# A residual product over 128 samples: the second last sample is stored in four transfers of 49, 64, 8 and 7 rows instead of one of 128

## The chip, the cores and the metric

The kernel runs on one core of a Trainium2 chip. The metric is the device time of one execution in microseconds (us); the time before is the median of three runs. A profiled execution of the kernel stands beside them: its span runs from the first to the last instruction that the profiler recorded. The core has 16 DMA engines that move data between HBM and the on-chip memory (SBUF), and they are used by transfers that SyncE (SP) and ScalarE (ACT) issue. A transfer adds 16 to a semaphore when all of it has landed.

## The reference

For each of 128 samples a 128x1024 matrix `x[b]` is multiplied by one of eight 128x128 weight matrices, chosen by an index, and added to itself:

```python
def reference(x, itok_B_0_7, L0_cond_weights):   # x (128, 128, 1024) f32
    ...
    w = weights[subjects]                        # (128, 128, 128)
    out = jnp.einsum('bct,bcd->bdt', x, w)
    ...
    x = x + _L0_cond_ref(x, itok_B_0_7, L0_cond_weights)
    return x
```

Each sample is 512 KB in and 512 KB out, so 67 MB are read and 67 MB written.

## The kernel before, in words

The samples are taken in `NT` = 32 groups of four (`H` = 2 pairs of `G` = 2 samples). Group `i` lies in slot `i % 12` of twelve SBUF buffers `xs`, as 128 partitions (rows) of 4 x 1024 floats; one row of one sample is 4 KB. It is an order written out by hand, with semaphores:

- SP issues one load for each sample (`load`, through `transfer`, L57), in the order of the samples. From group 12 on it waits until the slot's former group has been stored.
- GpSimd (POOL) copies the weight matrix that the index names (L196), TensorE makes four products of 128x512 for each pair (L206), and VectorE adds the pair's product in PSUM to `xs` in place (L217) and raises `s_added`.
- ACT issues the stores (`store`, L57), in the order of the groups. Groups 1 to 30 are stored whole, 2 MB in one transfer; group 0 in two pairs of 1 MB; group 31, the last, in three: its first pair (samples 124 and 125, 1 MB), then sample 126 (512 KB), and, after the big critical section and on ACT's queue too, sample 127 (L231, 512 KB).

Sample 126 is left alone by the expression `q1 - (b == B - 1)` in the last turn of the loop, which takes sample 127 out of the pair's store; the last transfer is issued outside, since the end of the program waits for it. SP meanwhile runs through a list of waits (L227 to L229), one for each of the last twelve slots and one for group 31's first pair, and then the program's closing instructions.

A store of 128 rows is carried by all 16 DMA engines, each of which works off what the two queues (SP's loads and ACT's stores) have for it.

Of the kernel before, what the change touches and what calls it, by code (L numbers as in the profile page):

```python
# [30 lines left out]
G = 2  # L31
H = 2
# [3 lines left out]
SLOTS = 12  # L36
# [5 lines left out]
DMA = 16  # L42

IDLE = 3

ROWS = 4
QUEUES = {mybir.EngineType.SP: "qSPDynamicHW", mybir.EngineType.Activation: "qActDynamicHW"}
# [2 lines left out]
def transfer(nc, engine, out, in_):  # L50

    later, nc._always_lower_symbolic_ap = nc._always_lower_symbolic_ap, False
    ins, outs = engine.lower_ap_dma(in_), engine.lower_ap_dma(out)
    nc._always_lower_symbolic_ap = later
    return engine.add_instruction(  # L57
        mybir.InstDMACopy(
            name=nc.get_next_instruction_name(),
            engine=engine.engine,  # L60
            ins=ins,
            outs=outs,
            mode="Copy",
            cce_op=ALU.bypass,
            queue=QUEUES[engine.engine],
        )
    )


@with_exitstack  # L70
def kernel(
    ctx: ExitStack,
    tc: tile.TileContext,
    x: bass.AP,
    subjects: bass.AP,
    weights: bass.AP,
    out: bass.AP,
):
    nc = tc.nc
    B, C, T = x.shape  # L80
    S, _, D = weights.shape
    NT = B // (G * H)

    def sbuf(name, *shape, dtype=F32):
        return ctx.enter_context(nc.sbuf_tensor(name, list(shape), dtype)).ap()

    given, near, wrap, index = (
        sbuf(name, 1, B, dtype=I32) for name in ("given", "near", "wrap", "index")
    )
    w_all = sbuf("w_all", C, S, D)  # L90
    ws = [sbuf(f"w{i}", C, 1, D) for i in range(W_SLOTS)]
    zeros = sbuf("zeros", C, N)
    xs = [sbuf(f"x{i}", C, H * G, T) for i in range(SLOTS)]
    ps = [
        ctx.enter_context(nc.psum_tensor(f"ps{i}", [D, G, T], F32)).ap() for i in range(P_SLOTS)
    ]

    s_given = tc.alloc_semaphore("s_given")
    s_wall = tc.alloc_semaphore("s_wall")
    s_index = tc.alloc_semaphore("s_index")  # L100
    s_zeros = tc.alloc_semaphore("s_zeros")
    s_copied = tc.alloc_semaphore("s_copied")
    s_product = tc.alloc_semaphore("s_product")
    s_added = tc.alloc_semaphore("s_added")

    s_pair = [[tc.alloc_semaphore(f"s_pair{i}_{h}") for h in range(H)] for i in range(SLOTS)]


    s_first = tc.alloc_semaphore("s_first")

    def emptied(i, h):

        turns = i // SLOTS
        return (DMA * G + (DMA if h == H - 1 else 0)) * turns

    def loaded(i, q):

        h = q // G
        return s_pair[i % SLOTS][h], emptied(i, h) + DMA * G

    def load(engine, i, q):
        k, h = i % SLOTS, q // G
        transfer(
            nc,
            engine,
            xs[k][:, q, :],
            x[i * H * G + q].rearrange("(a r) t -> a (r t)", r=ROWS),
        ).then_inc(s_pair[k][h], DMA)

    def store(i, q0, q1):  # L130
        k, b = i % SLOTS, i * H * G
        transfer(
            nc,
            nc.scalar,
            out[b + q0 : b + q1].rearrange("g d t -> d g t"),
            xs[k][:, q0:q1, :].rearrange("d (o g) t -> d o (g t)", g=min(G, q1 - q0)),
        ).then_inc(s_first if i == 0 and q1 == G else s_pair[k][(q1 - 1) // G], DMA)

    with tc.tile_critical():  # L139

        nc.scalar.dma_start(given, subjects.rearrange("(o b) -> o b", o=1)).then_inc(s_given, DMA)

        nc.vector.memset(zeros, 0.0).then_inc(s_zeros, 1)  # L143
        nc.tensor.wait_ge(s_zeros, 1)
        for _ in range(IDLE):
            nc.tensor.matmul(  # L146
                ps[P_SLOTS - 1][:, G - 1, :N], zeros[:, :D], zeros, start=True, stop=True
            )

        nc.vector.wait_ge(s_given, DMA)
        nc.vector.tensor_scalar(near, given, -S, S - 1, ALU.max, ALU.min).then_inc(s_index, 1)  # L153
        nc.vector.wait_ge(s_index, 1)
        nc.vector.tensor_scalar(wrap, near, 0, S, ALU.is_lt, ALU.mult).then_inc(s_index, 1)  # L155
        nc.vector.wait_ge(s_index, 2)
        nc.vector.tensor_tensor(index, near, wrap, ALU.add).then_inc(s_index, 1)  # L157
        nc.gpsimd.wait_ge(s_index, 3)


        nc.sync.dma_start(w_all, weights.rearrange("s c d -> c s d")).then_inc(s_wall, DMA)  # L161
        for i in range(NT):
            k = i % SLOTS
            if i == SLOTS:
                nc.sync.wait_ge(s_first, DMA)
            if i >= SLOTS:
                nc.sync.wait_ge(s_pair[k][H - 1], emptied(i, H - 1))
            for q in range(H * G):
                load(nc.sync, i, q)


        for j in range(NT * H):
            i, q0, q1 = j // H, j % H * G, (j % H + 1) * G
            k = i % SLOTS
            p = ps[j % P_SLOTS]

            ahead = j < P_SLOTS
            if ahead:  # L180
                nc.tensor.wait_ge(*loaded(i, q0))
            for q in range(q0, q1):
                b = i * H * G + q
                if b % R == 0:
                    _, subject = nc.values_load_multi_w_load_instructions(
                        index[0:1, b : b + R],
                        engines=[mybir.EngineType.Pool],
                        min_val=0,
                        max_val=S - 1,
                        skip_runtime_bounds_check_because="the index is clamped on the chip above",  # L190
                    )
                if b == 0:
                    nc.gpsimd.wait_ge(s_wall, DMA)
                if not ahead and q == q0:
                    nc.gpsimd.wait_ge(s_added, j - P_SLOTS + 1)
                copy = nc.gpsimd.tensor_copy(  # L196
                    ws[b % W_SLOTS], w_all[:, bass.ds(subject[b % R], 1), :]
                )
                if not ahead and q == q0:
                    copy.wait_op(*loaded(i, q0), "sem-ge")  # L200
            copy.then_inc(s_copied, 1)

            nc.tensor.wait_ge(s_copied, j + 1)
            for q in range(q0, q1):
                for t in range(0, T, N):
                    mm = nc.tensor.matmul(  # L206
                        p[:, q % G, t : t + N],
                        ws[(i * H * G + q) % W_SLOTS][:, 0, :],
                        xs[k][:, q, t : t + N],
                        start=True,  # L210
                        stop=True,
                    )
            mm.then_inc(s_product, 1)

            mine = xs[k][:, q0:q1, :]
            nc.vector.wait_ge(s_product, j + 1)
            nc.vector.tensor_tensor(  # L217
                mine, p, mine, ALU.add
            ).then_inc(s_added, 1)

            if i == 0 or q1 == H * G or i == NT - 1:
                nc.scalar.wait_ge(s_added, j + 1)
                store(i, q0 if i in (0, NT - 1) else 0, q1 - (b == B - 1))

    with tc.tile_critical() as waits:  # L227
        for i in range(NT - SLOTS, NT):
            nc.sync.wait_ge(s_pair[i % SLOTS][H - 1], emptied(i + SLOTS, H - 1))  # L229
        nc.sync.wait_ge(s_pair[(NT - 1) % SLOTS][0], emptied(NT - 1 + SLOTS, 0) + DMA)  # L230
    last = nc.scalar.dma_start(out[B - 1], xs[(NT - 1) % SLOTS][:, H * G - 1, :])  # L231

    tc.add_manual_dep(
        last.ins,
        waits.name,
        mybir.DependencyInfo(mybir.DependencyClass.NoSync, mybir.DependencyReason.SCHED_ONLY),
        reason="the end of the program waits for it",
    )
# [27 lines left out]
```

## Time and profile before

| | us |
|---|---|
| median of 3 runs | 327.0 (326.23 to 327.02) |
| span of the profiled execution | 325.4 |
| last add of VectorE ends | 278.7 |
| L231, the last store, is issued | 305.0 |
| last store has landed | 324.4 |
| TensorE busy | 241.1 (74%) |
| VectorE busy | 147.9 (45%) |
| bytes moved | 134.85 MB, mean 414 GB/s |

The page divides the span into 40 slices of 8.1 us; a digit is the busy share in tenths. The DMA line is the mean over the core's 16 DMA engines, so that one busy engine alone shows as 0.06 in a table with two decimals. The queue numbers of the page are q1 for SP's transfers and q10 for ACT's; q8 and q14 fetch instructions. Of the stores the page lists the size and the median time from issue to landing:

```profile
out_dram<-x ACTq DMA_DIRECT2D x30, 2048.0 KB, 47.3
out_dram<-x ACTq DMA_DIRECT2D x3, 1024.0 KB, 13.9
out_dram<-x ACTq DMA_DIRECT2D x2, 512.0 KB, 21.1
```

The two transfers of 512 KB are those of samples 126 and 127. A transfer waits in the queue behind the earlier ones, which is why its time to landing is long beside its size.

### The profile page before, as it was taken

How to read it: one execution, taken by the hardware profiler on the slowest of the kernel's cores; microseconds unless marked ns; L12 is line 12 of the kernel's file. 1: busy time of each engine (PE TensorE's matmuls, PEld its weight loads, DVE VectorE, ACT ScalarE, POOL GpSimd, SP SyncE). 2: the span in 40 equal slices, each digit the busy share in tenths (PEclk: the TensorE clock that was granted, in tenths of full speed). 3: DMA queues.
4: the chain of work that ended last, by engine and by line, in shares of the span. 5: the costliest groups of instructions: out<-in, count | busy, mean ns of one | idle time of the engine just before them, and what ended most of it. 6: DMA issues, size and time to landing. Idle time of an engine off the chain costs nothing.

```text
span 325.4 us, 1606 instructions
## 1 busy us (share of the span) xinstructions
PE 241.1 (74%) x518; PEld 95.2 (29%) x518; DVE 147.9 (45%) x68; POOL 34.3 (11%) x132
## 2 busy tenths in 40 slices
PE   6999988988888888888888888888888689000000
PEld 2444332333333333333333333333333233000000
DVE  1375754555555555454555555554554544200000
POOL 1011111011111111111011111111111010000000
PEclk9999999999999999999999999999999889655555
DMA  6999999999999999999999999999999999999994
GB/s 250 413 418 421 428 425 422 420 428 427 426 421 427 429 415 427 424 431 423 423 435 417 416 432 424 428 417 428 433 419 424 418 437 415 429 425 427 426 428 201
DMA packets 16074, 134.85 MB, mean 414 GB/s; under 512 B 2625, under 2 KB 3650, under 8 KB 3906
## 3 DMA queue, kind: packets, MB, share of 16 engines
q1 hardware_dynamic: 7184, 67.64, 49.7%
q10 hardware_dynamic: 8882, 67.11, 49.1%
q8 instruction: 4, 0.07, 0.1%
q14 instruction: 4, 0.03, 0.0%
HBM read 67.63 MB, written 67.11 MB: 414 GB/s over the span
## 4 chain that ended last, share of the span: by engine, by line
PE 42%; DVE 20%; issue 16%; POOL 4%; DMA 2%; POOLq 1%; SPq 0%
PE ps L206 42%; DVE x L217 20%; POOL w L196 4%; DMA x<-in_x_dram 2%; POOLq L196 1%; SPq L57 0%; SPq L161 0%; POOLq L139 0%; SPq L262 0%; SPq L139 0%
## 5 line engine op out<-in xcount | busy, mean ns | idle before, releaser
L206 PE MATMUL ps<-x,w 128*128 128x512 f32 x512 | 236.1, 607 | 33.6 <-POOL w L196 32.1
L217 DVE TENSOR_TENSOR x<-ps,x 128x2048 f32<-128x2048 f32 x64 | 146.7, 2292 | 129.1 <-PE ps L206 129.1
L206 PEld LDWEIGHTS ps<-x,w 128*128 128x128 f32 x512 | 93.3, 191 | 176.6 <-issue 93.9
L196 POOL COPY w<-w_all 128x128 f32 x128 | 34.1, 296 | 238.0 <-DMA x<-in_x_dram 207.7
L146 PE MATMUL ps<-zeros 128*128 128x512 f32 x6 | 5.0, 992 | 1.7 <-DVE zeros L143 1.7
L146 PEld LDWEIGHTS ps<-zeros 128*128 128x128 f32 x6 | 1.8, 328 | 3.7 <-issue 2.1
L143 DVE MEMSET zeros<- 128x512 f32 x1 | 0.5, 485 | 1.1 <-SPq L139 1.1
L153 DVE TENSOR_SCALAR near<-given 1x128 int32<-1x128 int32 x1 | 0.2, 215 | 0.6 <-DMA given<-in_itok_B_dram 0.6
L157 DVE CUSTOM_DVE_ANT_0 index<-near,wrap 1x256 uint16<-1x256 uint16 x1 | 0.3, 278 | 0.0
L155 DVE TENSOR_SCALAR wrap<-near 1x128 int32<-1x128 int32 x1 | 0.2, 216 | 0.0
L253 POOL MEMSET const-float32-0.0<- 128x1 f32 x1 | 0.1, 99 | 0.2 <-issue 0.2
L253 POOL MEMSET const-bfloat16-1.0<- 128x1 bf16 x1 | 0.1, 102 | 0.0
L253 POOL MEMSET const-uint8-127<- 128x1 uint8 x1 | 0.1, 102 | 0.0
L253 POOL MEMSET const-float32-1.0<- 128x1 f32 x1 | 0.1, 99 | 0.0
## 6 DMA issues: line engine op xcount, KB each, us to landing
x<-in_x_dram SPq DMA_DIRECT2D x128, 512.0 KB, 32.3
out_dram<-x ACTq DMA_DIRECT2D x30, 2048.0 KB, 47.3
out_dram<-x ACTq DMA_DIRECT2D x3, 1024.0 KB, 13.9
out_dram<-x ACTq DMA_DIRECT2D x2, 512.0 KB, 21.1
w_all<-in_L_cond_weights_dram SPq DMA_DIRECT2D x1, 512.0 KB, 4.5
given<-in_itok_B_dram ACTq DMA_DIRECT2D x1, 0.5 KB
```

Of the source, the lines that this page charges most:

```text
L143: nc.vector.memset(zeros, 0.0).then_inc(s_zeros, 1)
L146: nc.tensor.matmul(ps[P_SLOTS - 1][:, G - 1, :N], zeros[:, :D], zeros, start=True, stop=True)
L153: nc.vector.tensor_scalar(near, given, -S, S - 1, ALU.max, ALU.min).then_inc(s_index, 1)
L155: nc.vector.tensor_scalar(wrap, near, 0, S, ALU.is_lt, ALU.mult).then_inc(s_index, 1)
L157: nc.vector.tensor_tensor(index, near, wrap, ALU.add).then_inc(s_index, 1)
L196: copy = nc.gpsimd.tensor_copy(ws[b % W_SLOTS], w_all[:, bass.ds(subject[b % R], 1), :])
L206: mm = nc.tensor.matmul(p[:, q % G, t : t + N], ws[(i * H * G + q) % W_SLOTS][:, 0, :], xs[k][:, q, t : t + N], start=True, stop=True,)
L217: nc.vector.tensor_tensor(mine, p, mine, ALU.add).then_inc(s_added, 1)
L253: nc = _bacc.Bacc("TRN2", target_bir_lowering=False, num_devices=1)
```

## The change

Sample 126 is no longer stored by `store` but by four calls of a new function `store_rows`, one behind the other on ACT, of rows 0 to 48, 49 to 112, 113 to 120 and 121 to 127. They count on a semaphore of their own, `s_shares`, which SP waits for at the end in place of the slot's. The bytes and the place of the transfers in ACT's order stay.

```diff
+SHARES = 49, 64, 8, 7
...
+    s_shares = tc.alloc_semaphore("s_shares")
...
+    def store_rows(i, q, d0, d1):
+        return transfer(
+            nc,
+            nc.scalar,
+            out[i * H * G + q, d0:d1],
+            xs[i % SLOTS][d0:d1, q, :],
+        )
...
             if i == 0 or q1 == H * G or i == NT - 1:
                 nc.scalar.wait_ge(s_added, j + 1)
-                store(i, q0 if i in (0, NT - 1) else 0, q1 - (b == B - 1))
+                if b < B - 1:
+                    store(i, q0 if i in (0, NT - 1) else 0, q1)
+                else:
+                    d = 0
+                    for rows in SHARES:
+                        store_rows(i, q0, d, d + rows).then_inc(s_shares, DMA)
+                        d += rows
...
-        for i in range(NT - SLOTS, NT):
+        for i in range(NT - SLOTS, NT - 1):
             nc.sync.wait_ge(s_pair[i % SLOTS][H - 1], emptied(i + SLOTS, H - 1))
+        nc.sync.wait_ge(s_shares, DMA * len(SHARES))
         nc.sync.wait_ge(s_pair[(NT - 1) % SLOTS][0], emptied(NT - 1 + SLOTS, 0) + DMA)
     last = nc.scalar.dma_start(out[B - 1], xs[(NT - 1) % SLOTS][:, H * G - 1, :])
```

## The prediction

> **What bounds the kernel now.** I read the page's slices first. The core's 16 DMA engines are busy in every slice from the second to the last but one, while TensorE stops seven slices before the end:
>
> ```profile
> PE   6999988988888888888888888888888689000000
> ...
> DMA  6999999999999999999999999999999999999994
> GB/s 250 413 418 421 428 425 422 420 428 427 426 421 427 429 415 427 424 431 423 423 435 417 416 432 424 428 417 428 433 419 424 418 437 415 429 425 427 426 428 201
> ```
>
> The reader is to see that 134.85 MB go through engines that have no free time, and that from about 278 us only stores are left. What arithmetic costs does not matter; the time is bytes over rate plus how unevenly the engines finish. So I went to the end with the busy table in short windows (us, four compute engines, TensorE clock, mean busy share of the 16 DMA engines, GB/s):
>
> ```profile
> 319.75:320.00 0.25, 0.00 (x0) 0.00 (x0) 0.00 (x0) 0.00 (x0) 0.50 0.99 410
> ...
> 320.50:320.75 0.25, 0.00 (x0) 0.00 (x0) 0.00 (x0) 0.00 (x0) 0.50 0.69 279
> 320.75:321.00 0.25, 0.00 (x0) 0.00 (x0) 0.00 (x0) 0.00 (x0) 0.50 0.44 180
> ...
> 321.75:322.00 0.25, 0.00 (x0) 0.00 (x0) 0.00 (x0) 0.00 (x0) 0.50 0.17 66
> 322.00:322.25 0.25, 0.00 (x0) 0.00 (x0) 0.00 (x0) 0.00 (x0) 0.50 0.04 16
> 322.25:322.75 0.50, 0.00 (x0) 0.00 (x0) 0.00 (x0) 0.00 (x0) 0.50 0.06 25
> 322.75:324.00 1.25, 0.00 (x0) 0.00 (x0) 0.00 (x0) 0.00 (x0) 0.50 0.06 26
> 324.00:324.40 0.40, 0.00 (x0) 0.00 (x0) 0.00 (x0) 0.00 (x0) 0.50 0.00 0
> ```
>
> A share of 0.06 is one engine of sixteen (1/16 = 0.0625). All work until about 320.3; more than half are done by 321; from about 322.1 one engine alone moves bytes, until 324.0. Call it the late engine. It sets the end: 324.0, then 0.4 us until its last semaphore lands, then 1.0 us of closing instructions, 325.4. Third, the DMA view from 322.25 to the end, 40 slices of 0.079 us:
>
> ```profile
> DMA  1010101010101010101010000000000000000000
> GB/s 52 0 52 0 52 0 52 0 52 0 52 0 52 0 52 0 52 0 52 0 52 0 0 0 0 0 0 0 0 0 0 0 0 0 0 0 0 0 0 0
> DMA packets 13, 0.05 MB, mean 14 GB/s; under 512 B 2, under 2 KB 2, under 8 KB 13
> ```
>
> Eleven rows of 4 KB start one behind another every two slices (0.158 us), and two 4-byte semaphore packets lie among them. Eight rows are the engine's share of sample 127 (128 rows over 16 engines), the three before them the end of its share of sample 126. The boundary between the two transfers leaves no gap. A row costs 1.25 us / 8 = 0.156 us. Last, the issues:
>
> ```profile
> 262.14 42.32 ACTq L57 DMA_DIRECT2D out_dram<-x  x8
> ...
> 305.02 0.54 ACTq L231 DMA_DIRECT2D out_dram<-x  x1
> ```
>
> ACT has issued everything by 305.6, more than 14 us before the first engine runs dry.
>
> **The change, part by part.** *Bytes and order.* Nothing is computed otherwise, and loads, matmuls and adds stay. Sample 126 still goes between the first half of group 31 and sample 127, on the same queue; only which engine carries which of its 128 rows can change. Before, each carries 8.
>
> *How the parts fall.* No transfer of 49, 64, 8 or 7 rows is in the trace. I bound it from both sides: (a) rows spread over all 16 as evenly as they go, about 8 each, change nothing, 0 us; (b) each odd transfer on one engine puts 49+4+1+1 = 55 rows on that one, 47 more than before, 47 x 0.156 = 7.3 us on it. Between them (c): equal parts on the largest number of engines, up to 16, that divides the rows, counted from the first: 7 engines with 7 rows, 16 with 4, 8 with 1, 7 with 1. I take (c), because the trace's 128-row transfers are in equal parts of 8. Then engines 0 to 6 carry 13 rows, engine 7 five, engines 8 to 15 four; 7x13 + 5 + 8x4 = 128. [...]
>
> *What that costs.* On engines 8 to 15: -4 rows, -4 x 0.156 = -0.62 us; on engine 7: -3 rows, -0.47 us; on 0 to 6: +5 rows, +0.78 us, and three more semaphore packets. For those: 322.25 to 324.0 is 1.75 us for 11 rows (1.72 us) and two semaphore packets, about 0.01 us each; +0.03, together +0.81 us. If the late engine is one of 8 to 15, its end moves from 324.00 to 323.38. The next one stops near 322.15 (share 0.04 in 322.00 to 322.25); if it is among the first seven it goes to 322.96 and stays hidden by 0.42 us. Were that cover gone, the end would be set there.
>
> *Issues.* ACT issues four transfers for one. The last issue, which waits for no room in its queue, took 0.54 us; three more cost 1.6 us, so L231 may start at 306.7 for 305.02. The queue covers it: it holds work until 320.3 on the earliest engine. Behind it on ACT stands only L231 and the end; SP has finished its loads by 261.7. Cost 0; without the cover 1.6 us.
>
> *A fixed price per transfer.* From below 0 (the unbroken row of starts above); from above, the 0.4 us that the last semaphore took to land, once for each of three added transfers, 1.2 us. I take 0: the row that is the same thing shows no gap. [...]
>
> *Waits.* SP waits at the end for as many semaphores as before, one of them now the shares' own. It is reached when the late engine has done its four rows, 0.62 us earlier like all it does afterwards, and eight rows (1.25 us) are still to come; no wait is put behind. Cost 0.
>
> Sum: -0.62 us on a span of 325.4, 324.8. The median of the runs is 327.0, 1.6 us above this execution's span; I keep that distance: **326.4 us**.
>
> **The rivals.**
> *B, the late engine is one of the first seven (slower).* Then its own queue grows: 324.00 + 0.81, and the time is 327.8. No view names an engine, so the rows do not exclude it; by count it is 7 of 16. It decides from any case in which the engine that ends last holds 13 rows. [...]
> *C, the 49 rows go to one engine.* That engine, done between 320.3 and 322.1 today, ends 7.3 us later, 327.6 to 329.4 for 324.0: 330.6 to 332.4 us. Against it: the equal parts that the rows show.
> *D, the rows slow one another.* Today engine and rows fit the same way in every store; the parts pair them differently. If each of the 13 rows took twice its 0.156 us, the first seven would end 2.0 us later still, 322.96 + 2.0 = 324.98, 1.0 us behind today: 328.0. If half of them did, 323.97: no change, 327.0. For it: only that nothing like it is in the trace. Against it: near 424 GB/s with loads and stores mixed.
> *E, the rows spread evenly after all (a).* 327.0, no change.
>
> **How the numbers follow.** About 0.3% (1.0 us) is what a measurement of this kernel can tell from no change; the three runs lie 0.8 us apart. I give C 0.06, D and E together 0.09. The other 0.85 is shared by count, 9 engines to 7: the forecast 0.48, B 0.37. The forecast's own range is 325.8 to 327.0 (0.62 us, give or take about the spread of the runs). Faster by over 0.3% needs 0.36 us more than I work out, about half that spread, and the lateness in executions without a profile is unknown: 0.45 of the forecast, 0.22. Slower by over 0.3%: B's 0.81 us is 0.2 short of the bound; 0.37 of B is 0.14, C is 0.06, and 0.01 of D: 0.21. The rest, 0.57, is within 0.3%. The range 325.7 to 328.0 takes in the forecast, B and D's upper end and leaves out C and the tails.
>
> **What would show it.** In the changed kernel's profile the 0.06 stretch at the end should be shorter by 0.5 to 0.7 us, with 8 + 4 rows on the late engine, and the share just before it higher, as seven engines work 0.8 us longer; the total packets should be those of before and some semaphore packets more (7+16+8+7 = 38 for 16). A lone stretch that is longer by 0.8 us is B; 55 rows on one engine is C; rows further apart than 0.156 us while several engines are at work is D. L231 issued after 320 would make the issue sum wrong, and gaps between the parts the price of a transfer.

## The result: 0.7% slower

The changed kernel takes 329.1 us (median of 6 runs, 328.22 to 329.48) against 326.8 us for the kernel before (6 runs), a ratio of 1.0069 with a 95% interval of 1.0058 to 1.008: 2.3 us more. The page of the profile after, with the lines that answer to those of before:

```profile
span 327.1 us, 1609 instructions
...
DMA  6999999999999999999999999999999999999993
GB/s 255 413 409 428 427 424 420 432 418 430 422 428 427 426 424 419 432 416 432 425 426 421 424 429 420 426 425 427 424 428 426 429 417 425 430 425 425 430 420 115
DMA packets 16096, 134.85 MB, mean 412 GB/s; under 512 B 2647, under 2 KB 3672, under 8 KB 3928
...
out_dram<-x ACTq DMA_DIRECT2D x1, 256.0 KB
out_dram<-x ACTq DMA_DIRECT2D x1, 196.0 KB
out_dram<-x ACTq DMA_DIRECT2D x1, 32.0 KB
```

Bytes and rate are those of before up to the last slice, and there are 22 packets more (16,096 for 16,074): 38 semaphore packets of the four parts for 16 of the one transfer, as equal parts on 7, 16, 8 and 7 engines give. All the difference lies in the last few us: the last 2 MB store landed at 318.8 us, in the kernel before at 319.5. The busy table of the changed kernel there (stretch in us, four compute engines, TensorE clock, DMA share, GB/s):

```profile
318.00:319.00 1.00, 0.00 (x0) 0.00 (x0) 0.00 (x0) 0.00 (x0) 0.50 1.05 434
319.00:320.00 1.00, 0.00 (x0) 0.00 (x0) 0.00 (x0) 0.00 (x0) 0.50 0.93 356
320.00:321.00 1.00, 0.00 (x0) 0.00 (x0) 0.00 (x0) 0.00 (x0) 0.50 0.66 209
321.00:322.00 1.00, 0.00 (x0) 0.00 (x0) 0.00 (x0) 0.00 (x0) 0.50 0.47 180
322.00:323.00 1.00, 0.00 (x0) 0.00 (x0) 0.00 (x0) 0.00 (x0) 0.50 0.22 70
323.50:325.75 2.25, 0.00 (x0) 0.00 (x0) 0.00 (x0) 0.00 (x0) 0.50 0.06 25
```

And the same table of the kernel before:

```profile
319.00:320.00 1.00, 0.00 (x0) 0.00 (x0) 0.00 (x0) 0.00 (x0) 0.50 1.04 426
320.00:321.00 1.00, 0.00 (x0) 0.00 (x0) 0.00 (x0) 0.00 (x0) 0.50 0.76 311
321.00:322.00 1.00, 0.00 (x0) 0.00 (x0) 0.00 (x0) 0.00 (x0) 0.50 0.36 147
322.25:324.00 1.75, 0.00 (x0) 0.00 (x0) 0.00 (x0) 0.00 (x0) 0.50 0.06 26
```

Divide the last column by the one before it. Before, a full share moves 410 GB/s in every row (426/1.04, 311/0.76, 147/0.36). After, it moves 383 in 319 to 320 and in 321 to 322, 317 in 320 to 321 and 318 in 322 to 323: engines are busy and move less. That is a second effect besides the late engine, which now works alone until about 325.8 for 324.0.

What the late engine does alone is seen in the DMA view of the changed kernel from 323.3 to 326.0, 40 slices of 0.068 us:

```profile
DMA  0010101001010100101001010101001010100000
...
DMA packets 21, 0.06 MB, mean 23 GB/s; under 512 B 6, under 2 KB 6, under 8 KB 21
```

The packets of the trace can also be followed back, each to the one that ended just before it on its engine. Written with D for 8 KB (two rows, 311 ns), r for one row (4 KB, 159 ns) and a bar for a semaphore packet, the late engine's last packets are, in the two kernels:

```
before  DDDDDDDD|rrrrrrrr|rrrrrrrr|
after   DDDDDD(420 ns)D(428 ns)D(927 ns)|rrr(333 ns)r(691 ns)rrr|rrrr|r|r|rrrrrrrr|
```

In the changed kernel it has a part of 7, one of 4, one of 1 and one of 1: 13 rows of sample 126 for 8. So it is one of the seven engines that take a share of the 49 rows. Five of its packets are longer than their kind, three of 8 KB and two rows, by 1.55 us together. Over the last stretch of the stores (from 312 us) 20 packets were over a tenth longer than their kind (slow packets from here on), by 4.55 us together over all engines; in the kernel before, not one of 602.

### The profile page after: what moved, and what is told of

Read it like the earlier page. It is cut to its first block, busy times and chain, and to the rows that moved or that the text cites. A ratio compares the mean times of both kernels' runs of the same rounds, so it can differ in the third digit from the quotient of the medians.

```text
span 327.1 us, 1609 instructions
## 1 busy us (share of the span) xinstructions
PE 242.0 (74%) x518; PEld 95.7 (29%) x518; DVE 147.9 (45%) x68; POOL 34.3 (10%) x132
## 2 busy tenths in 40 slices
DMA packets 16096, 134.85 MB, mean 412 GB/s; under 512 B 2647, under 2 KB 3672, under 8 KB 3928
## 4 chain that ended last, share of the span: by engine, by line
PE 43%; DVE 19%; issue 16%; POOL 4%; DMA 2%; POOLq 1%; SPq 0%
PE ps L217 43%; DVE x L228 19%; POOL w L207 4%; DMA x<-in_x_dram 2%; POOLq L207 1%; SPq L59 0%; SPq L172 0%; SPq L280 0%; SPq L150 0%
```

## The experiments

Two causes were to be told apart, called R and X in the expectations: **R**, five more rows on the engine that ends last; **X**, engines that slow one another because a part makes them read SBUF rows that another engine carries in a transfer of 128 (crossing). The rivals were **T**, a price for each added transfer, and **H**, slow writes to HBM or the splitting as such. All experiments alter only how sample 126 is stored; `SHARES` and `store_rows` are those of the changed kernel unless the diff says otherwise.

**Halves.** `e1_halves`:

```diff
-SHARES = 49, 64, 8, 7
+SHARES = 64, 64
```

> Sample 126 in two transfers of 64 rows: every engine carries 8 rows, as before the change, but rows of other partitions than in a transfer of 128. Theory R (the rows count: the late engine is one of the first seven and has 5 rows more, 0.81 us): no change within 0.3%, no slow packet. Theory X (crossing: engines that read rows which another engine carries in the 128-row transfers slow one another): packets over 0.16 us per 4 KB row in the last 6 us, and the late engine's end 0.6 to 1.5 us later, ratio 1.002 to 1.005. Theory T (a price for each added transfer): one more transfer, a third of what three cost, about 0.5 us.

326.7 us, ratio 1.0012 (1.0001 to 1.0024). 18 slow packets, 2.96 us together; on the late engine some 0.2 us. X is there at equal row counts, but its price was below what was expected: in this trace nearly all of it, 2.8 of 2.96 us, fell to other engines than the late one.

**Columns.** `e2_columns`:

```diff
-SHARES = 49, 64, 8, 7
+SHARES = 512, 512
...
-            out[i * H * G + q, d0:d1],
-            xs[i % SLOTS][d0:d1, q, :],
+            out[i * H * G + q, :, d0:d1],
+            xs[i % SLOTS][:, q, d0:d1],
```

> Sample 126 in two transfers of all 128 rows, 512 columns each: rows stay with their engines, only the transfers are more (two for one) and the rows are halves of 2 KB, 256 packets for 128. Theory X and theory R: no change within 0.3% (at most some hundredths of a us for each packet). Theory T (a price for each added transfer): about 0.5 us later and a gap between the parts on the late engine.

326.63 us, ratio 0.9999 (0.999 to 1.0009), no slow packet. The further transfer, each of the two with all 128 rows, cost nothing that shows (326.63 for 326.64 us): T falls.

**Names for the engines.** `e3_names`:

```diff
-SHARES = 49, 64, 8, 7
+SHARES = 96, 11, 6, 5, 4, 3, 2, 1
```

> Sample 126 in parts of 96, 11, 6, 5, 4, 3, 2 and 1 rows, so that the number of parts an engine takes names it: if a part falls in equal shares on the first engines, engine 0 shows 6,1,1,1,1,1,1,1 rows, engine 6 to 10 show 6,1 and the last five show 6 alone. Theory R: the late engine shows at least one single row besides (its index is 6 minus the number of single rows after 6,1), and is one of 0 to 6, as it was seen to carry 13 rows in the changed kernel. If the late engine differs from run to run, it may show any index.

One execution, 328.55 us, with 17 slow packets. The lone engine's last 2.5 us (323.1 to 325.6, slices of 0.063 us):

```profile
DMA  3000010100101001010010100101001010010000
...
DMA packets 19, 0.06 MB, mean 23 GB/s; under 512 B 5, under 2 KB 5, under 8 KB 19
```

14 rows and 5 semaphore packets: followed back they are `rrr|r|r|r|rrrrrrrr|`, the end of the part of 96, three single rows and sample 127. If a part on few engines falls on the first ones, the three singles are the parts of 11, 6 and 5 rows: the engine takes part in a transfer on five engines and not in one on four, and counted from 0 it is number 4. The packets of a trace name no engine, so the number rests on that order, which no trace shows.

**Even and odd rows.** `e4_even_odd` stores rows 0, 2, 4, ... and then 1, 3, 5, ..., in SBUF and in the output alike:

```diff
-SHARES = 49, 64, 8, 7
+SHARES = 0, 1
...
-            out[i * H * G + q, d0:d1],
-            xs[i % SLOTS][d0:d1, q, :],
+            out[i * H * G + q].rearrange("(d g) t -> d g t", g=2)[:, d0, :],
+            xs[i % SLOTS][d0:128:2, q, :],
...
-                        store_rows(i, q0, d, d + rows).then_inc(s_shares, DMA)
-                        d += rows
+                        store_rows(i, q0, rows, rows).then_inc(s_shares, DMA)
```

> Sample 126 in two transfers of 64 rows, the even rows and the odd rows: as many transfers and rows on each engine as with halves, but each transfer draws on all 128 partitions, not on one half of them. Theory X in the form that engines compete for the half of the memory that a part lies in: slow packets fewer and shorter than with halves, the end 0 to 0.6 us later. Theory X in the form that any crossing costs: as with halves. Theory T: as with halves, 0.5 us. Theory R: no change.

326.56 us, ratio 0.9997 (0.9987 to 1.0006), no slow packet. That two transfers of 64 rows have slow packets in one form and none in the other is against "the splitting as such".

For the rest, the parts choose their SBUF rows by a start and a step, while the output rows stay those of consecutive parts:

```diff
-    def store_rows(i, q, d0, d1):
+    def store_rows(i, q, d0, d1, p0, step):
...
-            xs[i % SLOTS][d0:d1, q, :],
+            xs[i % SLOTS][p0 : p0 + (d1 - d0 - 1) * step + 1 : step, q, :],
...
-                    for rows in SHARES:
-                        store_rows(i, q0, d, d + rows).then_inc(s_shares, DMA)
+                    for rows, p0, step in SHARES:
+                        store_rows(i, q0, d, d + rows, p0, step).then_inc(s_shares, DMA)
```

**The changed kernel's parts from rows that lie apart.** `e5_spread`, each part as (rows, start, step):

```diff
-SHARES = 49, 64, 8, 7
+SHARES = (49, 0, 2), (64, 1, 2), (8, 0, 16), (7, 8, 16)
```

> The changed kernel with one thing altered: its parts of 49, 64, 8 and 7 rows go to the same output rows, in the same order and number, but take their data from SBUF rows that lie apart (49 rows two apart, 64 rows two apart, 8 and 7 rows sixteen apart) and not in one block; the values in sample 126's output are therefore those of other rows. Theory R+X (5 rows more on the late engine, 0.8 us, and the rest of the 2.3 us from parts that lie in one block of SBUF): 0.6 to 1.2 us over the kernel before, ratio 1.002 to 1.004, few or no slow packets, the late engine still with 7, 4, 1, 1 and 8 rows. Theory H (the slow packets come from the writes to HBM, or from the splitting as such): as the changed kernel, ratio 1.006 to 1.008, and slow packets.

328.38 us, ratio 1.0054 (1.004 to 1.0068). More than expected: only part of X is gone. Four slow packets are left of 20, but two of them are the late engine's, the first two rows of its part of 7. Followed back, its packets from there to the end are `r(566 ns)r(682 ns)rrrrr|rrrr|r|r|rrrrrrrr|`. These two rows are 0.93 us over their kind; with 0.81 us for five rows more that is 1.74 of the 1.8 us measured. In a part of 49, rows two apart still brought slow packets.

**Halves of the output from even and odd SBUF rows.** `e6_halves_src`:

```diff
-SHARES = 49, 64, 8, 7
+SHARES = (64, 0, 2), (64, 1, 2)
```

> As the two halves of 64 rows, with the same output rows for each part, but the data of each part from every second SBUF row (sample 126's output has the values of other rows). Theory R+X: no slow packet and a ratio of 0.999 to 1.001. Theory H: slow packets as with the halves, a ratio of 1.001 to 1.002.

326.53 us, ratio 0.9998 (0.9988 to 1.0007), no slow packet. The output rows of each transfer are those of the halves, and only the SBUF side differs: the slow packets (18 with `e1_halves`, none here) come from which SBUF rows a part reads. H falls.

**Without and with engine 4.** `e7_k4` and `e8_k5`:

```diff
-SHARES = 49, 64, 8, 7
+SHARES = (64, 0, 2), (32, 1, 4), (4, 0, 20), (4, 64, 20), (4, 8, 20), (4, 52, 20), (4, 16, 20), (4, 40, 20), (4, 24, 20), (4, 32, 20)
```

> Parts of 64, 32 and eight times 4 rows, all from SBUF rows that lie apart (sample 126's output has the values of other rows). If the parts of 4 fall on engines 0 to 3, these carry 14 rows and all others 6. Theory R with the late engine number 4, as the run with many parts named it: the late engine has 2 rows fewer than 8, 0.31 us, ratio 0.998 to 1.000 if the small parts cost nothing; six of its rows in the trace. Rival (the late engine is one of 0 to 3, or changes from run to run): 14 rows on it, 0.93 us and more, ratio about 1.003. Theory T (a price for each of the nine added transfers): over 1 us later with six rows on it.

```diff
-SHARES = 49, 64, 8, 7
+SHARES = (64, 0, 2), (32, 1, 4), (25, 0, 5), (7, 8, 16)
```

> Parts of 64, 32, 25 and 7 rows, all from SBUF rows that lie apart (sample 126's output has the values of other rows). If the 25 fall on engines 0 to 4, these carry 6+5+1 = 12 rows, engines 5 and 6 seven, the rest six. Theory R with the late engine number 4: 4 rows more on it, 0.62 us, ratio 1.001 to 1.003, and 12 rows in the trace. Rival (the late engine is 5 or 6, or higher): 7 or 6 rows, ratio 0.999 to 1.000. This run and the one with parts of 4 differ, for engine 4, by 6 rows or 0.93 us.

326.38 us, ratio 0.9995 (0.9986 to 1.0004), and 327.5 us, ratio 1.0025 (1.0016 to 1.0034). In the first the late engine shows 4 and 2 rows and no part of 4; in the second it has the part of five engines. So by the same count it is number 4 in these runs too. The two kernels differ by 0.30% of 326.6, 1.0 us, for six rows (0.93 us). The second cost somewhat more than its four rows, 0.8 us for 0.62. The late engine takes only two of the first kernel's ten transfers; what many transfers on one engine cost is read from `e10_own4`, next.

**The same row counts without crossing.** `e9_own8` and `e10_own4` test two ideas of which rows are an engine's own, eight neighbours or two blocks of four neighbours that lie 32 rows apart, with 13, 5 and 4 rows on the engines as in the changed kernel:

```diff
-SHARES = 49, 64, 8, 7
+SHARES = (7, 0, 8), (7, 1, 8), (7, 2, 8), (7, 3, 8), (7, 4, 8), (7, 5, 8), (7, 6, 8), (64, 0, 2), (8, 7, 8), (7, 1, 8)
```

> The rows of the changed kernel without its crossing, if an engine's own rows in a transfer of 128 are eight neighbours: the 49 rows as seven transfers of 7 rows that lie eight apart, so that engine e takes row 8e + r, the 64 as every second row, the 8 and the 7 as rows eight apart; engines 0 to 6 again carry 13 rows, engine 7 five, the others four (sample 126's output has the values of other rows). Theory R+X (rows 0.8 us, the rest of the 2.3 us by crossing): no slow packet, 0.8 to 1.0 us over the kernel before, ratio 1.0025 to 1.003. Theory R alone, with a price for each odd transfer (ten of them): as the changed kernel or slower, 1.006 to 1.012.

```diff
-SHARES = 49, 64, 8, 7
+SHARES = (7, 0, 4), (7, 1, 4), (7, 2, 4), (7, 3, 4), (7, 32, 4), (7, 33, 4), (7, 34, 4), (64, 0, 2), (8, 3, 4), (7, 35, 4)
```

> [...] If an engine's own rows are eight neighbours, this crosses: slow packets, ratio 1.004 to 1.008. If they are two blocks of four, this is the run without slow packets, 1.0025 to 1.003, and the run with rows eight apart is the slower.

Eight neighbours: 327.66 us, ratio 1.0038 (1.0024 to 1.0052), with 8 slow packets. Two blocks of four: 327.43 us, ratio 1.0024 (1.0015 to 1.0033), and none. The times alone don't part the two; the packets do. The busy table of the second:

```profile
319.00:320.00 1.00, 0.00 (x0) 0.00 (x0) 0.00 (x0) 0.00 (x0) 0.50 1.01 410
320.00:321.00 1.00, 0.00 (x0) 0.00 (x0) 0.00 (x0) 0.00 (x0) 0.50 0.73 295
321.00:322.00 1.00, 0.00 (x0) 0.00 (x0) 0.00 (x0) 0.00 (x0) 0.50 0.43 172
322.00:323.00 1.00, 0.00 (x0) 0.00 (x0) 0.00 (x0) 0.00 (x0) 0.50 0.20 82
323.00:324.75 1.75, 0.00 (x0) 0.00 (x0) 0.00 (x0) 0.00 (x0) 0.50 0.06 26
```

A full share moves 400 to 410 GB/s in every row, as in the kernel before, though the late engine has its 13 rows. This is R alone: 0.24% of 326.6, 0.8 us. The late engine takes all ten transfers, one row of each but four of the 64, and the time is that of its five added rows: the nine added transfers cost nothing that the interval, 0.3 us either way, can show.

**Sixteen rows at a time.** `e11_sixteens` and `e12_sixteens_apart`, eight rows on each engine as before:

```diff
-SHARES = 49, 64, 8, 7
+SHARES = (16, 0, 1), (16, 16, 1), (16, 32, 1), (16, 48, 1), (16, 64, 1), (16, 80, 1), (16, 96, 1), (16, 112, 1)
```

> Sample 126 in eight transfers of 16 neighbouring rows each: every engine carries 8 rows as in the kernel before, one of each part, and 16 engines at a time draw on 16 rows that belong to two to four engines in a transfer of 128. Theory X: far more slow packets than with halves, the end 1 to 9 us later, ratio 1.003 to 1.03. Theory R: no change, as the row counts are those of before. Theory T (a price for each of seven added transfers): as the next run.

```diff
-SHARES = 49, 64, 8, 7
+SHARES = (16, 0, 8), (16, 1, 8), (16, 2, 8), (16, 3, 8), (16, 4, 8), (16, 5, 8), (16, 6, 8), (16, 7, 8)
```

> Sample 126 in eight transfers of 16 rows that lie eight apart: as many transfers and rows on each engine as the run before it, but engine e takes row 8e + r (sample 126's output has the values of other rows). Theory X with neighbours as own rows: no slow packet, ratio 0.999 to 1.001. Theory T: slower, like the run with neighbouring rows.

327.8 us, ratio 1.004 (1.0027 to 1.0054), and 326.77 us, ratio 1.0009 (0.9999 to 1.002). Each has 20 slow packets, 3.94 and 3.71 us together, so by X rows eight apart are not the engines' own rows; that expectation failed with `e9_own8`'s. But neighbouring rows alone, with no row more on any engine, cost 0.4%; how many engines' own rows sixteen neighbours are was not shown. From the table of the first, where 344/1.01 is 341 GB/s for a full share:

```profile
319.00:320.00 1.00, 0.00 (x0) 0.00 (x0) 0.00 (x0) 0.00 (x0) 0.50 1.01 344
320.00:321.00 1.00, 0.00 (x0) 0.00 (x0) 0.00 (x0) 0.00 (x0) 0.50 0.89 328
```

What seems to decide is whether the late engine meets slow packets. Followed back, its last 8 KB packets took 455 and 688 ns in the first; in the second, an 8 KB packet of 422 ns and a few slow rows fell to other engines. This part of the reading rests on one trace each. The ten times of the second fit it: eight are 326.69 to 326.98 us, the other two 327.76 and 327.89.

## Why the prediction was wrong, by its own steps

*What bounds the kernel* was right: one engine alone sets the end, and all of the change shows in its last packets.

*How the parts fall* was right: the 38 semaphore packets of the four parts and the late engine's 7, 4, 1 and 1 rows are those of (c), and the late engine's rows in `e3_names`, `e7_k4`, `e8_k5` and `e10_own4` fit equal parts too. That the parts begin with the first engine is in no trace and remained an assumption. *A row's 0.156 us* was right: the late engine's lone rows start 0.154 to 0.156 us apart on average in the changed kernel, `e3_names`, `e8_k5` and `e10_own4`.

*Which engine is late* was the first step that failed, in the paragraph on the numbers: the chance was shared by count, nine engines to seven, and the sign of the forecast hung on it. It is one of the seven that the change loads with five more rows, as its 13 rows show, and number 4 by the count of `e3_names`. No run shows the term of -0.62 us, four rows fewer on the late engine: by the prediction's own working it is +0.81 for that case (rival B), and `e10_own4` measures 0.8 us for it.

*Rows that slow one another* (rival D) was the second step, and the larger part of the time. It was priced well enough, at up to 2.0 us on the first seven engines, and given a chance of 0.09 together with E because "nothing like it is in the trace". Before, every store takes all 128 rows, and not one of the 602 packets of its last stretch is slow, so that trace could not show it. It also stood as an alternative to B, and the two add up: 2.3 us in all less the 0.8 us of the rows leave 1.5 us. The late engine's packets in the one profile give the same size: from the landing of the last 2 MB store to the end it takes 7.38 us for 4.96 before, 2.42 more: 0.81 are rows, 1.55 the five long packets. The range ended at 328.0 since no case held both.

Which rows are an engine's own the runs don't settle. Parts of rows four apart that start in rows 0 to 3 and 32 to 35 brought no slow packet (`e10_own4`), rows eight apart 8 (`e9_own8`) and 20 (`e12_sixteens_apart`) of them; but parts of 64 even and odd rows have none either (`e4_even_odd`, `e6_halves_src`). Which rows an engine takes there was not measured.

*Issues* cost nothing, as forecast, though their own price was set too low. ACT spent 4.0, 1.0, 0.9 and 0.9 us on the four parts, 2.8 us for the three added ones where 1.6 was worked out, and issued the last store at 307.18 (306.7 was forecast; 305.02 and 1.6 make 306.6). The queue held work well beyond that:

```profile
250.16 56.38 ACTq L59 DMA_DIRECT2D out_dram<-x  x12
307.18 0.39 ACTq L249 DMA_DIRECT2D out_dram<-x  x1
```

*A fixed price per transfer* of 0 was right: `e2_columns` adds one transfer and is not to be told from the kernel before, and `e10_own4` adds nine on the late engine and costs what its rows cost. Nine of its ten transfers are of 7 and 8 rows (28 and 32 KB) and stand in a filled queue.

No version here beat the kernel before. If the parts fall on the first engines, as the prediction assumed, every transfer that reaches engine 5 loads engine 4 as much, so only engines 0 to 3 can take rows off it; two rows fewer (`e7_k4`) are 0.31 us by the rows, within the interval of no change. Why the late engine is late was not tested, nor how the engines hold one another up: the runs show that the choice of SBUF rows does it, not by what.

## What to carry to other kernels

When one DMA engine ends last, find out which one before moving rows: here parts in sizes of a known pattern (11, 6, 5, 4, 3, 2, 1 rows) gave its number in one profile, on the assumption that a part on few engines falls on the first ones (`e3_names`). A transfer of fewer rows changed two things at once here, how many rows each engine has and which SBUF rows it reads, and the second cost about twice the first (1.5 us for 0.8). Check it by dividing GB/s by the DMA share: in these runs a share that moved less than elsewhere (317 for 410 GB/s) went with slow packets (20 for none).

## What the runs showed of the hardware that was not expected

- A transfer of n rows went in equal parts to k engines, as far as the late engine's rows and the semaphore packets show: 49 to 7, 8 to 8, 7 to 7, 25 to 5, and 4 to 4. The page counts 22 packets more than before for the changed kernel, 28 for `e8_k5` and 48 for `e7_k4`, as semaphore packets of 7+16+8+7, 16+16+5+7 and 16+16+8x4 engines give for the 16 of one transfer.
- Which SBUF rows a store took decided here whether its packets were slow: in the changed kernel 4 KB packets took up to 0.69 us for 0.16 and an 8 KB packet 0.93 for 0.31, and with as many rows on each engine but other SBUF rows none was slow (`e10_own4`). Two halves have 18 slow packets, the same output rows from other SBUF rows none (`e6_halves_src`).
- Ten transfers for one in a filled queue, nine of them of 7 or 8 rows, cost the late engine nothing beyond their rows that the interval, 0.3 us either way, can show: 0.8 us for five rows more (`e10_own4`). Of ACT's time the three added ones of the changed kernel took 0.9 to 1.0 us each.
